# Row sums of one adjacency on ScalarE instead of TensorE, and the last two batches' h turned by exchange instead of by transposes

## The chip, the cores and the metric

The kernel runs on one core of a Trainium2 chip. The metric is the device time of one execution in microseconds (us). The engines are called as in the profile: PE is TensorE's matmul, PEld its weight load, ACT is ScalarE, DVE is VectorE, POOL is GpSimd, SP is SyncE, which here only issues DMAs (SPq in the profile).

## The reference

There are B = 16 graphs of N = 1024 nodes with C = 128 features, a 0/1 symmetric adjacency `adj[b]` for each, and L = 4 layers in each of two blocks.

```
# block 0: gated graph layers
h = relu(layernorm(x))
for i in 0..3:
    m = adj[b] (summed over nodes) of h @ weight[i]
    r = sigmoid(W_ir m + b + W_hr h + b);  z = sigmoid(W_iz m + b + W_hz h + b)
    n = tanh(W_in m + b + r * (W_hn h + b))
    h = (1 - z) * n + z * h
x = x + h * nodemask
# block 1: graph convolutions
h = relu(layernorm(x))
for i in 0..3:
    h = relu(adj[b] @ (h @ W[i]) + b[i])
    h = gamma[i] * (h - mean) * rsqrt(var + eps) + beta[i]     # over all batches and nodes
x = x + h
```

## The kernel before

Features lie on the 128 partitions and nodes along a row wherever a layer works (`hT`, 128x1024), nodes lie on the partitions where the layernorm works (`xt`, 8 blocks of 128x128). A product with the adjacency is written in two parts, a rounded high part of its operand and the rest, so one `aggregate` of a batch has 32 matmuls of 128x512 (L525): 8 rows of the adjacency, by two parts, by two halves of the nodes, into two PSUM banks.

**First phase** (block 0). Two streams, `sa` for the even batches and `sb` for the odd ones, take turns in `half_step(one, two)`. In each half step `one` aggregates (tiles `pm`) while `two` goes through its gates (`gate_step`, twelve pairs of matmuls at L969 into `g_r`, `g_hn`, `g_xn`, `g_z`, then sigmoid, tanh and the update of h on ACT and DVE). At the end of an aggregate, ACT copies both banks to `m` (L944). A counter `clock` starts at 3 and goes up by one in each half step. Side jobs are put in an agenda by `at(n, place, job)` and issued by `due(place)` in half step n; those of the place "gap" are issued in the middle of the aggregate. `plan` puts there, for one batch, the tail of the previous one and the preparation of the next. The order of all engines is written by hand for the first two half steps; for the rest of the phase only that of PE, POOL and SP is, and in the second phase a scheduler makes the order of all engines.

A batch's rows of the adjacency are loaded from the input as 32-bit values into `stage`, rounded into `row` tiles (`sa.rows` and `sb.rows`), and looked at for values that are not 0 or 1 by ACT: `glance` (L587) copies a row into `junk` while an accumulator sums it into `low`. POOL and a transposing DMA write the transposed adjacency in 16 bits to DRAM, `adjT_d[b]`, for the second phase.

**Tail of a batch.** h lies with features on the partitions, x with nodes. For all but the last two batches, `blocks_out` turns each half of h by one DVE transpose of 32x32 blocks (L711) into a `t_out` half tile and stores it by one SP DMA in DRAM (`cross_out`); a half step later `exchange_in` brings it back by four SP DMAs of 64 KB, which puts the blocks in their places; `tail_sums` adds it to x from SBUF, with the node mask (L732), and takes the layernorm's sums; `y_mid` is the normalized x (L674), and both go to DRAM (`xmid_d`, `ymid_d`). For batches 14 and 15, `last_tail` does it without the exchange: `tail_sums` has PE transpose the eight 128x128 blocks of h into PSUM (`pt_x`, L726), DVE adds from there, and `store_xmid` follows. What is left, `rest()`, is the normalizing and the store of y. For batch 14 `sa.rest()` is issued behind the last gates of batch 15, for batch 15 `sb.rest()` behind the second phase's first `first_weights`.

**Second phase** (block 1). Layer 0 runs over the 16 batches in order. `load_adjT` (L1229) loads eight rows of 256 KB each by SP DMAs, for an even batch into the one `block` tile, for an odd batch into `packed` half tiles, a ring of eight buffers that the first phase uses for `t_out`, `t_h` and the like. Each row is then widened to 32 bits (`wide`) by ACT (rows 1, 4 and 7, L1232) or by DVE (the others, L1234). `first_split` loads y from `ymid_d` and makes its high part on ACT (`chw`, L1291) and the rest on DVE (L1292). `aggregate` fills the banks `pc_m` (even batches) or `pc_g_r`, `pc_g_z` (odd ones), and `first_weights` of the batch before stands in TensorE's order between the aggregate's two halves or behind it: ACT copies the banks to `cm` (L1301), PE multiplies by the weights (`pw`, L1302), ACT makes `feat` (L1281). `work2` is a pool of the second phase that takes the place of the first phase's `work`, and `cm` is its first tile.

For the layers 1 to 3, batch 0 uses the sums of its adjacency's rows, `degree` (128x1024, the same in each partition, kept in the space of `w_mT`), in `raw_weights`. `row_sums` makes them on PE as a product of a matrix of ones with batch 0's `wide` rows (`pt_deg`, L1328), 16 matmuls behind batch 0's aggregate in the code, and ACT copies them from PSUM (L1332).

Of the kernel before, what the change touches and what calls it, by code (L numbers as in the profile page):

```python
# [8 lines left out]
F32 = mybir.dt.float32  # L9
F32R = mybir.dt.float32r  # L10
BF16 = mybir.dt.bfloat16
U16 = mybir.dt.uint16
I32 = mybir.dt.int32
AF = mybir.ActivationFunctionType
ALU = mybir.AluOpType
AX = mybir.AxisListType
P = 128
HALF = 512
# [323 lines left out]
def exact_path(  # L342
# [21 lines left out]
    nc = tc.nc  # L364
    B, N, C = x.shape
    L = g_weight.shape[0]
    NB = N // P
    NH = N // HALF
    BH = HALF // P
    assert C == P  # L370

    const = ctx.enter_context(tc.tile_pool(name="const", bufs=1))
# [9 lines left out]
    def tmp(name):  # L382
        return ps_t.tile([P, HALF], F32, tag="tmp", name=name)

    adjT_d = [dram.tile([NB, P, N], BF16, tag=f"adjT{b}", name=f"adjT_d{b}") for b in range(B)]
    xmid_d = [dram.tile([N, C], F32, tag=f"xmid{b}", name=f"xmid_d{b}") for b in range(B)]
    ymid_d = [dram.tile([P, N], F32, tag=f"ymid{b}", name=f"ymid_d{b}") for b in range(B)]

    def flat(name):
        return keep.tile([P, NB, C], F32, tag="x", name=name, bufs=4)  # L390
# [19 lines left out]
    nc.vector.memset(ones, 1.0)  # L410
    low = const.tile([P, (B + 2) * NB], F32, tag="low", name="low")
    nc.vector.memset(low, 0.0)

    w_c = const.tile([P, L, C], F32, tag="w_c", name="w_c")
    w_mT = const.tile([P, L, 3 * C], F32, tag="w_mT", name="w_mT")
# [118 lines left out]
    with ExitStack() as st:  # L534
# [46 lines left out]
        def glance(b, stage, js):  # L581

            junk = work.tile([P, N], BF16, tag="junk", name=f"junk{b}_{js[0]}", bufs=1)
            for j in js:
                lows = stage[j % 4].bitcast(U16).rearrange("p (n t) -> p n t", t=2)[:, :, 0]
                k = b * NB + j
                nc.scalar.activation(junk, lows, AF.Copy, accum_out=low[:, k : k + 1])  # L587

        def exchange_out(t, name):
            d = rawd.tile([P, HALF], F32, tag="cross", name=f"cross_{name}", bufs=8)  # L590
            nc.sync.dma_start(d, t)
            return d

        def exchange_in(d, t):

            src = d.rearrange("(t r) (s x) -> s r t x", t=4, s=4)
            for s in range(4):
                nc.sync.dma_start(t[s * 32 : (s + 1) * 32, :].rearrange("r (t x) -> r t x", t=4), src[s])  # L598
# [84 lines left out]
        def norm_apply(xt, y, nt):  # L683
            norm_root(nt, 0, NB)
            norm_scale(nt, 0, NB)
            norm_blocks(xt, y, nt, range(NB))
# [13 lines left out]
        def by_nodes(cols):  # L700
            return cols.rearrange("c (q k i) -> c k q i", q=4, i=32)

        def four_ways(cols):
            return cols.rearrange("p (k a c) -> p k a c", a=4, c=32)

        def blocks_out(src, name):

            return [half_out(cross_tile(f"t_{name}_{hf}"), src, hf, name)[0] for hf in range(NH)]
# [5 lines left out]
        def cross_tile(name):  # L714
            return half_tile(name).bitcast(F32)

        def tail_sums(b, xt, hT, parts=None):

            for hf in range(NH):
                if parts:  # L720
                    pt = by_nodes(parts[hf])
                else:
                    pt = tmp(f"pt_x{b}_{hf}")
                    for q in range(BH):
                        k = hf * BH + q
                        nc.tensor.transpose(pt[:, q * P : (q + 1) * P], hT[:, k * P : (k + 1) * P], ident)  # L726
                    pt = four_ways(pt)
                for q in range(BH):
                    k = hf * BH + q
                    xk = xt[:, k, :].rearrange("p (a c) -> p a c", a=4)  # L730
                    mask = maskT[:, b * NB + k : b * NB + k + 1]
                    nc.vector.scalar_tensor_tensor(xk, pt[:, q, :, :], mask, xk, ALU.mult, ALU.add)  # L732
            return norm_stats(xt, f"mid{b}")
# [5 lines left out]
        def y_mid(b):  # L739
            return work.tile([P, N], F32, tag="h", name=f"y_mid{b}", bufs=7)  # L740

        def store_xmid(b, xt):
            nc.gpsimd.dma_start(xmid_d[b].rearrange("(k p) c -> p k c", p=P), xt)
# [2 lines left out]
            nc.gpsimd.dma_start(ymid_d[b], y)  # L746

        def last_tail(b, xt, hT):
            nt = tail_sums(b, xt, hT)
            y = y_mid(b) if b + 1 < B else xt.rearrange("p k c -> p (k c)")  # L750
            store_xmid(b, xt)

            def rest():
                norm_apply(xt, y, nt)
                store_ymid(b, y)

            return rest
# [10 lines left out]
        class Stream:  # L768
# [53 lines left out]
            def plan(self, n, tail=None):  # L822

                if tail:
                    b, xt, hT, parts = tail
                    end = {}

                    def sums():
                        end["norm"] = tail_sums(b, xt, hT, parts)

                    def blocks():
                        end["y"] = y_mid(b)
                        norm_blocks(xt, end["y"], end["norm"], range(NB))

                    at(n + 2, "gap", sums)
                    at(n + 3, "mid", lambda: store_xmid(b, xt))
                    at(n + 3, "gap", lambda: norm_factors(end["norm"]))
                    at(n + 4, "gap", blocks)
                    at(n + 5, "mid", lambda: store_ymid(b, end["y"]))
                if self.b + 2 < B:  # L840
                    at(n + 5, "mid", self.next_load)
                    at(n + 5, "gap", self.next_sums)
                    at(n + 6, "gap", self.next_factors)
                    at(n + 7, "gap", self.next_blocks)
# [180 lines left out]
        def at(n, place, go):  # L1025
            agenda.setdefault((n, place), []).append(go)
# [5 lines left out]
        def half_step(one, two, gated=None, halfway=None):  # L1032

            feed.next_step()
            one.split = []
            if one.i == 0:
                two.fetch()
            due("ins")
            if one is sb and one.i == 0 or written[0] and one is sa:
                feed.jobs = transposes([(s.b, s.rows) for s in (sa, sb)])  # L1040
            if one.i > 0:
                one.split_step()
                two.fetch()
                feed.some(2)
            two.gate_step(0)
            two.half_away(0)
            two.first_four()
            if feed.full or (clock[0], "mid") in agenda:

                pace = small.tile([P, 1], F32, tag="pace", name=f"pace{clock[0]}")  # L1050
                nc.gpsimd.tensor_copy(pace, two.new[:, :1])
                feed.store()
                due("mid")
            due("outs")
            one.split_back(0, two.last_act, two.mid_dve)
            one.split_back(1, two.last_act, two.mid_dve)
            if one.i > 0:
                feed.some(1)
            two.gate_step(1, None, one.split)
            two.half_away(1)  # L1060
            with behind(two.first_act):
                due("late")
            if one.i == 0:
                feed.some(1)
            two.last_four()
            if gated:
                gated()
            if one.i == 0:
                with behind(two.last_m):
                    one.split_step()  # L1070
            one.agg_step(0)
            if halfway:
                halfway()
            with behind(two.last_act, two.last_dve, *one.split):
                due("gap")
            feed.some(NB if written[0] and one is sa else 1)
            one.agg_step(1)
            two.finish()
            clock[0] += 1
# [3 lines left out]
        with tc.tile_pool(name="prep", bufs=1) as prep, tc.manual_schedule(engines=every):  # L1083
# [106 lines left out]

            sa.plan(0)
            sb.plan(1)
            half_step(sa, sb, looks, lambda: turn_layer(prep, w_g, 1))
            join_layer(1)
            half_step(sb, sa, None, lambda: turn_layer(prep, w_g, 2))
# [124 lines left out]
            nc.tensor.matmul(pc[hf], w_c[:, i, :], mt[:, cols], start=True, stop=True)  # L1320
        conv_done(0, i, pc, stats)

    def row_sums(rows):

        pd = [tmp(f"pt_deg{hf}") for hf in range(NH)]
        for j in range(NB):
            for hf in range(NH):
                nc.tensor.matmul(  # L1328
                    pd[hf], ones_r, rows[j][:, hf * HALF : (hf + 1) * HALF], start=(j == 0), stop=(j == NB - 1)
                )  # L1330
        for hf in range(NH):
            nc.scalar.copy(degree[:, hf * HALF : (hf + 1) * HALF], pd[hf])  # L1332

    xo = []

    def pieces(b):
# [28 lines left out]
            for n0, n in pieces(k):  # L1365
                nc.gpsimd.dma_start(xo_piece(k, n0, n), by_node(xmid_d[k], n0, n))

    ones_r = work.tile([P, P], F32R, tag="ones_r", name="ones_r", bufs=1)
    nc.vector.tensor_copy(ones_r, ones.to_broadcast([P, P]))
    degree = w_mT.rearrange("p l c -> p (l c)")[:, :N]  # L1370

    stats = small.tile([P, B * NH, 6], F32, tag="bn_st", name="stats0")
# [1 line left out]
    for b in range(B):  # L1374
        rows = load_adjT(b, 0)
        hw_next = first_split(b + 1) if b + 1 < B else None
        pm = banks(b, 0)
        aggregate(pm, hw, rows, 0)
        if waiting:
            last = first_weights(*waiting, stats)  # L1380
            if b == 1:
                with tc.issue_after(last.ins):
                    sb.rest()
        if b == B - 1:
            hw_next = raw_split(1)
        aggregate(pm, hw, rows, 1)
        if b == 0:
            row_sums(rows)
        hw, waiting = hw_next, (b, pm)


# [110 lines left out]
```

## Time and profile before

| what | us |
|---|---|
| median of three runs | 1797.83 (1797.73 to 1798.45) |
| profiled execution | 1797.0 |
| its span | 1795.1 |
| PE busy | 1762.7 |
| ACT busy | 1108.3 |
| DVE busy | 1259.4 |
| POOL busy | 389.0 |

The mean clock granted to TensorE was 0.997 of full speed. The profiled execution has 1.9 us around its span and lies 0.83 us below the median of the runs. The first phase takes the span up to about 1175 us, the second the rest; the first layer of the second phase takes 9.02 us a batch from batch 2 on.

In the lines of a timeline or chain the first number is the start in the span, the second the duration, both in us; brackets hold the idle time of the engine before it and what ended it. Neighbouring instructions of one kind are one line (x8).

### The profile page before, as it was taken

Reading aid. Unit: us, or ns where it says so; the run is one execution under the profiler, and the core shown is the slowest. Engines: PE = TensorE matmul, PEld = TensorE weight load, DVE = VectorE, ACT = ScalarE, POOL = GpSimd, SP = SyncE. Lnnn points to the kernel's source line nnn. Section 1 sums busy time; section 2 is a strip of 40 time slices with the busy share of each in tenths; the row PEclk is TensorE's granted clock in tenths of the full one; section 3 lists DMA queues with packets and bytes.
Section 4 is the critical chain, followed back from the end, with each engine's and each line's share of the span. In section 5 each row is a group of like instructions: output and inputs, shape, how many; then the busy total and the mean of one; then the engine's idle time right before and its main releaser. Section 6 shows DMA issues by size and latency. Waiting matters only on the chain.

```text
span 1795.1 us, 22286 instructions
## 1 busy us (share of the span) xinstructions
PE 1762.7 (98%) x6742; PEld 1194.2 (67%) x6742; DVE 1259.4 (70%) x2307; ACT 1108.3 (62%) x1717; POOL 389.0 (22%) x417
## 2 busy tenths in 40 slices
PE   9999999999999999999999999999999999999997
PEld 6555555565566555656555655677778888888886
DVE  7567867877776776877686766676666666666665
ACT  5346557466556555655655645477777767768765
POOL 3213423332332331422332333010100000000010
PEclk9999999999999999999999999999999999999999
DMA  6447777676676766766866767778866565757666
GB/s 252 113 127 263 190 206 245 197 214 212 213 208 217 230 192 196 255 201 175 284 175 187 246 197 211 270 270 309 280 220 246 205 247 207 255 214 251 230 227 255
DMA packets 363968, 399.11 MB, mean 222 GB/s; under 512 B 159820, under 2 KB 240496, under 8 KB 363840
## 3 DMA queue, kind: packets, MB, share of 16 engines
q1 hardware_dynamic: 343088, 322.54, 56.9%
q0 software_dynamic: 20224, 74.80, 11.5%
q8 instruction: 55, 0.90, 0.2%
q14 instruction: 73, 0.60, 0.1%
q10 hardware_dynamic: 528, 0.26, 0.0%
HBM read 266.95 MB, written 96.99 MB: 203 GB/s over the span
## 4 chain that ended last, share of the span: by engine, by line
PE 81%; DMA 5%; DVE 5%; ACT 4%; issue 2%; SPq 2%; DVEq 0%; ACTq 0%
PE pm L525 20%; PE pc_m L525 13%; PE g_z L969 10%; PE g_r L969 9%; PE pc_g_z L525 6%; PE pc_g_r L525 6%; PE g_xn L969 5%; PE g_hn L969 5%; PE hw_c L500 4%; DMA cross_in<-t_in 1%; ACT y_in L674 1%; SPq L598 1%; DMA stage<-in_adj_dram 1%; DMA cross_h<-t_h 1%; PE pw_g_hn L1302 1%
## 5 line engine op out<-in xcount | busy, mean ns | idle before, releaser
L525 PE MATMUL pm<-row,ghw 128*128 128x512 f32 x2048 | 505.3, 403 | 10.7 <-ACT ghw L905 10.6
L525 PEld LDWEIGHTS pm<-row,ghw 128*128 128x128 f32 x2048 | 384.3, 188 | 123.1 <-issue 26.3
L525 PE MATMUL pc_m<-wide,chw 128*128 128x512 f32 x1024 | 246.0, 395 | 0.0
L609 POOL CAST half<-row 128x1024 bf16<-128x1024 f32 x128 | 147.9, 1163 | 329.0 <-DMA adjT<-half 314.2
L525 PEld LDWEIGHTS pc_m<-wide,chw 128*128 128x128 f32 x1024 | 190.4, 188 | 42.3 <-issue 4.3
L988 ACT ACTIVATE z<-g_z,brz 128x512 f32<-128x512 f32 x128 | 87.5, 684 | 172.6 <-PE g_z L969 172.3
L525 PE MATMUL pc_g_r<-wide,chw 128*128 128x512 f32 x464 | 186.9, 403 | 0.3 <-ACT chw L502 0.3
L578 POOL CAST row<-stage 128x1024 fp32r<-128x1024 f32 x112 | 132.9, 1196 | 241.0 <-DMA stage<-in_adj_dram 194.9
L525 PE MATMUL pc_g_z<-wide,chw 128*128 128x512 f32 x464 | 181.0, 390 | 0.0
L982 DVE SCALAR_TENSOR_TENSOR r<-g_hn,vecs,r 128x512 f32<-128x512 f32 x128 | 95.1, 743 | 121.4 <-ACT r L981 76.6
L944 ACT COPY m<-pm 128x512 f32<-128x512 f32 x128 | 68.5, 587 | 151.6 <-PE pm L525 151.6
L1234 DVE CAST wide<-block 128x1024 fp32r<-128x1024 bf16 x160 | 109.9, 692 | 73.2 <-PE pc_m L525 48.3
L1234 DVE CAST wide<-packed 128x1024 fp32r<-128x1024 bf16 x160 | 110.2, 691 | 72.0 <-PE pc_g_z L525 53.9
L987 ACT ACTIVATE r<-r,vecs 128x512 f32<-128x512 f32 x128 | 91.8, 717 | 100.7 <-DVE r L983 100.5
L994 DVE TENSOR_TENSOR h<-h,r 128x512 f32<-128x512 f32 x96 | 81.3, 847 | 98.4 <-ACT r L987 98.4
L1232 ACT CAST wide<-packed 128x1024 fp32r<-128x1024 bf16 x96 | 100.6, 1048 | 59.0 <-PE pc_m L525 26.6
L969 PE MATMUL g_r<-m,w_mT 128*128 128x512 f32 x256 | 131.3, 594 | 3.5 <-ACT m L944 3.2
L1232 ACT CAST wide<-block 128x1024 fp32r<-128x1024 bf16 x96 | 100.6, 1048 | 52.3 <-PE pc_g_z L525 27.7
L969 PE MATMUL g_xn<-m,w_mT 128*128 128x512 f32 x256 | 130.7, 592 | 0.0
L969 PE MATMUL g_z<-m,w_mT 128*128 128x512 f32 x256 | 130.7, 592 | 0.0
L995 DVE TENSOR_TENSOR h<-h,z 128x512 f32<-128x512 f32 x128 | 116.3, 912 | 4.6 <-ACT z L988 1.5
L1282 DVE BATCH_NORM_STATS2 stats<-feat 128x6 f32<-128x512 f32 x128 | 84.1, 686 | 47.0 <-ACT feat L1281 45.9
(186 smaller groups left out, 2808.2 us busy)
## 6 DMA issues: line engine op xcount, KB each, us to landing
block<-adjT_d SPq DMA_DIRECT2D x256, 256.0 KB, 4.7
packed<-adjT_d SPq DMA_DIRECT2D x256, 256.0 KB, 5.6
stage<-in_adj_dram SPq DMA_DIRECT2D x120, 512.0 KB, 5.1
adjT_d<-adjT POOLq DMA_DIRECT2D x16, 2048.0 KB, 8.3
cross_h<-t_h SPq DMA_DIRECT2D x90, 256.0 KB, 3.0
n_h<-cross_h SPq DMA_DIRECT2D x360, 64.0 KB, 2.0
xmid_d<-x POOLq DMA_DIRECT2D x16, 512.0 KB, 5.3
y<-ymid_d POOLq DMA_DIRECT2D x16, 512.0 KB, 5.3
```

The source lines that it names most:

```text
L525: nc.tensor.matmul(pm[hf], hw[s][:, j * P : (j + 1) * P], rows[j][:, hf * HALF : (hf + 1) * HALF], start=(j == 0 and s == 0), stop=(j == N ...
L578: nc.gpsimd.tensor_copy(t, stage[j % 4])
L609: nc.gpsimd.tensor_copy(t, row.bitcast(F32))
L969: nc.tensor.matmul(po, wT[:, i, g * C : (g + 1) * C], rhs, start=start, stop=stop)
L982: nc.vector.scalar_tensor_tensor(r, phn, b_hn(i), r, ALU.add, ALU.mult)
L987: nc.scalar.activation(r, r, AF.Tanh, bias=b_in(i))
L988: self.last_act = nc.scalar.activation(z, pz, AF.Sigmoid, bias=brz[:, 3 * i + 1 : 3 * i + 2])
L994: nc.vector.tensor_sub(ho, hin, r)
L995: nc.vector.tensor_mul(ho, ho, z)
L1232: nc.scalar.copy(r, t)
L1234: nc.vector.tensor_copy(r, t)
L1282: nc.vector.bn_stats(stats[:, b * NH + hf, :], dst)
```

## The change

Row sums: for each of the first four half steps, two of batch 0's rows are summed by ACT in the "gap" place, by a copy into `junk` with an accumulator, into a column of `deg` each (128x8). In the fifth, a POOL DMA stores `deg` as 1024 values in DRAM, `degree_d`, and at batch 0 of the second phase a POOL DMA loads them into all partitions of `degree`. The product with ones, its operand and the copies from PSUM are gone.

Tails: `last_tail` turns h by `blocks_out`, as the tails of other batches do, and everything else (the exchange back, the additions, the sums, the stores) goes into `rest()`. The branch of `tail_sums` that transposes on PE is gone.

```diff
+    degree_d = dram.tile([1, N], F32, tag="degree", name="degree_d")
...
+    deg = const.tile([P, NB], F32, tag="deg", name="deg")
...
+        def row_sums(rows, js):
+
+            junk = work.tile([P, N], BF16, tag="junk", name=f"total{js[0]}", bufs=1)
+            for j in js:
+                nc.scalar.activation(junk, rows[j].bitcast(F32), AF.Copy, accum_out=deg[:, j : j + 1])
+
...
-        def tail_sums(b, xt, hT, parts=None):
+        def tail_sums(b, xt, parts):
 
             for hf in range(NH):
-                if parts:
-                    pt = by_nodes(parts[hf])
-                else:
-                    pt = tmp(f"pt_x{b}_{hf}")
-                    for q in range(BH):
-                        k = hf * BH + q
-                        nc.tensor.transpose(pt[:, q * P : (q + 1) * P], hT[:, k * P : (k + 1) * P], ident)
-                    pt = four_ways(pt)
+                pt = by_nodes(parts[hf])
...
         def last_tail(b, xt, hT):
-            nt = tail_sums(b, xt, hT)
-            y = y_mid(b) if b + 1 < B else xt.rearrange("p k c -> p (k c)")
-            store_xmid(b, xt)
+            outs = blocks_out(hT, f"out{b}")
+            parts = [hT[:, hf * HALF : (hf + 1) * HALF] for hf in range(NH)]
 
             def rest():
+                for d, t in zip(outs, parts):
+                    exchange_in(d, t)
+                nt = tail_sums(b, xt, parts)
+                y = y_mid(b) if b + 1 < B else xt.rearrange("p k c -> p (k c)")
+                store_xmid(b, xt)
                 norm_apply(xt, y, nt)
                 store_ymid(b, y)
...
+            for k in range(4):
+                js = range(2 * k, 2 * k + 2)
+                at(3 + k, "gap", lambda js=js: row_sums(sa.rows, js))
+            at(7, "gap", lambda: nc.gpsimd.dma_start(degree_d.rearrange("o (k p) -> p (o k)", p=P), deg))
             half_step(sa, sb, looks, lambda: turn_layer(prep, w_g, 1))
...
-    def row_sums(rows):
-
-        pd = [tmp(f"pt_deg{hf}") for hf in range(NH)]
-        for j in range(NB):
-            for hf in range(NH):
-                nc.tensor.matmul(
-                    pd[hf], ones_r, rows[j][:, hf * HALF : (hf + 1) * HALF], start=(j == 0), stop=(j == NB - 1)
-                )
-        for hf in range(NH):
-            nc.scalar.copy(degree[:, hf * HALF : (hf + 1) * HALF], pd[hf])
...
-    ones_r = work.tile([P, P], F32R, tag="ones_r", name="ones_r", bufs=1)
-    nc.vector.tensor_copy(ones_r, ones.to_broadcast([P, P]))
...
         if b == 0:
-            row_sums(rows)
+            nc.gpsimd.dma_start(degree, degree_d.rearrange("o n -> (o n)").partition_broadcast(P))
```

More of the change, by code (lines that the diff above doesn't have):

```diff
@@ L828, in sums @@
                     def sums():
-                        end["norm"] = tail_sums(b, xt, hT, parts)
+                        end["norm"] = tail_sums(b, xt, parts)
                     def blocks():
```

## The prediction

> **What bounds the kernel now.** I read the page first, for the engine that fills the span and the chain that ended last.
>
> ```profile
> PE 1762.7 (98%) x6742; PEld 1194.2 (67%) x6742; DVE 1259.4 (70%) x2307; ACT 1108.3 (62%) x1717; POOL 389.0 (22%) x417
> ...
> PE 81%; DMA 5%; DVE 5%; ACT 4%; issue 2%; SPq 2%; DVEq 0%; ACTq 0%
> ```
>
> TensorE is busy for 98% of the span and 81% of the chain lies on it. Work taken off TensorE shortens the kernel unless a new wait fills the hole, so each step below is a walk along TensorE's queue. Second, the tile view of `pt_deg`, the product with ones, and the chain of waits around the change of phase, near 1162 to 1189 us (start, us, what):
>
> ```profile
> L1328 PE MATMUL pt_deg<-wide,ones_r x16: 387/391/467, 1184.7 to 1188.3; 128*128 128x512 f32 x16
> ```
>
> ```profile
> 1162.05 0.87 PE pt_x L726 x8
> ...
> 1173.92 0.44 PE pt_x L726 x4
> ...
> 1176.68 0.43 PE pt_x L726 x4
> ...
> 1183.67 1.07 ACT cm L1301 x2
> 1184.74 3.91 PE pt_deg L1328 x16
> ```
>
> Everything that the change removes from TensorE is on the chain. Third, ACT's timeline, for the holes that take the new row sums and for the order of work after the change of phase (start, us, idle before it and its end in brackets):
>
> ```profile
> 59.58 1.07 ACT L944 COPY m<-pm 128x512 f32<-128x512 f32 x2 [3.17 <-PE pm L525]
> 80.43 1.07 ACT L944 COPY m<-pm 128x512 f32<-128x512 f32 x2 [3.18 <-PE pm L525]
> 102.82 1.07 ACT L944 COPY m<-pm 128x512 f32<-128x512 f32 x2 [6.38 <-PE pm L525]
> 120.39 1.07 ACT L944 COPY m<-pm 128x512 f32<-128x512 f32 x2 [3.95 <-PE pm L525]
> ...
> 1161.67 1.06 ACT L1291 CAST chw<-y 128x1024 fp32r<-128x1024 f32 x1 [2.12 <-PE pm L525]
> 1162.63 1.06 ACT L944 COPY m<-pm 128x512 f32<-128x512 f32 x2
> ...
> 1176.65 3.19 ACT L674 ACTIVATE y_mid<-x,ms_mid,rs_mid 128x128 f32<-128x128 f32 x8 [0.99 <-DVE ms_mid L670]
> 1181.35 1.05 ACT L1291 CAST chw<-y 128x1024 fp32r<-128x1024 f32 x1 [1.51 <-PE pc_m L525]
> ```
>
> Last, SP's timeline, because the new exchanges are issued there, among the loads of the second phase's rows:
>
> ```profile
> 1146.35 3.88 SPq L1229 DMA_DIRECT2D block<-adjT_d  x8
> 1150.63 6.09 SPq L1229 DMA_DIRECT2D packed<-adjT_d  x8
> 1158.43 3.83 SPq L1229 DMA_DIRECT2D block<-adjT_d  x8
> 1162.62 24.25 SPq L1229 DMA_DIRECT2D packed<-adjT_d  x8
> ```
>
> Now batch 1's rows (the first `packed` group) are asked for at 1150.6 to 1156.7, some 25 us before TensorE needs them at 1181.6. That cover is what the change spends.
>
> **Removed.** The row sums: 3.91 us of TensorE. The 16 transposes of `pt_x`: by their neighbours' starts in TensorE's timeline 0.88, 0.36 and 0.35, so 1.59 us. `pt_flag` (0.12 us) moves far forward, to a place near 1060 us where TensorE waits 2.8 us anyway. Gross ceiling 5.6 us. The cast of `ones_r` (0.30 us DVE) and the two ACT copies of `degree` (1.06 us) go too, in places where neither ends a wait of TensorE.
>
> **Added early: nothing.** A row sum is an ACT copy of 128x1024 with an accumulator; the nearest row is `junk` (L587, 1.047 us and 0.187 us for reading the accumulator), so two per gap take 2.5 us, in gaps where ACT idles 3.17, 3.18, 6.38 and 3.95 us. 0.7 us to spare: TensorE's aggregate hides them. Without that cover it would be up to 4 x 2.5 = 9.9 us; I take 0. The store of `degree_d` is one issue on POOL (0.89 us for `adjT_d` at 130.86) before an idle stretch of 14.84 us. The load waits for w_mT's first layers, free since about 1136 us, is one issue of some 0.6 us on POOL with only `xo` loads behind it, and is first used at 1333 us: 0. No row has 4-byte elements; the nearest, the 64 KB exchange pieces in runs of 512 B, land in 2.0 us (up to 8.9), and 1000 us lie between store and load.
>
> The Trainium skill's page "DMA: Bandwidth & Descriptors" (Specifications) wants 512 B or more for line rate and says that smaller pieces are read, modified and written; the page would make this store slow, which the 1000 us hide as well.
>
> **Moved: the tail of batches 14 and 15.** The order on each engine is known, since the changed program can be built; durations are from rows of before.
>
> *First* (batch 14's eight transposes, 0.88 us): they cover ACT, which casts `chw` (1.06) before it copies m. Without them the two `g_r<-h` matmuls end at 1162.74 while the first m is there at about 1163.2. So 0.5 comes back; 0.36 stays. `pc_m` of batch 0 loses 0.71 and 0.12 more and ends at 1181.61 - 1.19 = 1180.4.
>
> *Second* (SP's queue): behind the first block loads stand now batch 14's two stores and eight pieces, and, after the first of batch 1's `packed` rows, batch 15's two stores. These wait for DVE's transposes of h, whose second half is finished at 1175.5 to 1176.1 (L996) and then needs a place on a DVE that also does batch 14's sums, and 0.70 us for the transpose. Batch 1's rows 1 to 7 are issued only from about 1177.8 and land, at the median of 5.1 us for L1229 (2.4 to 7.7; I take 3.4, as only the first must be in), from 1181.2. ACT meanwhile runs y_mid of 14 (3.19 us, about 1177.9 to 1181.1) ahead of row 1's cast (1.05): ready at 1182.2. TensorE comes to row 1 at 1180.4 + 0.9 = 1181.3 and stands 0.9 us. At the best 0; at a landing of 7.7 us, 4. It ends batch 1's aggregate at 1182.2 + 28 x 0.227 = 1188.6.
>
> *Third* (the copy cm of batch 0, which empties the banks for batch 2's aggregate and feeds TensorE's `pw`): it now stands on ACT behind `chw` of batch 3, which starts at the end of batch 1's aggregate (1188.9 to 1190.0), and its buffer is released only when DVE's last addition of batch 15's h to x is done. DVE has those additions on both sides of its low part of `chw` (1.23): 1190.0 + 1.23 + 4 x 0.34 = 1192.6. Then half of cm (0.5) and a wake-up: `pw` starts at 1193.5 instead of 1188.6. TensorE stands 4.9 us; behind it are `pw` and the whole of batch 2. At the best, were cm to wait for `chw` alone, 1.9. At the worst, batch 15's stores land in 6.9 us, the median of `cross_out`, instead of 3.0, the median of `cross_h`, and its additions end 1 to 4 us later. I take the small end in both, since at this point the first phase's stage loads are over.
>
> The Trainium skill's page "DMA: Bandwidth & Descriptors" (Anatomy of one DMA) gives a transfer, there one issued by GpSimd, about 2.0 us of fixed time whatever its size, plus bytes/436e3; as an estimate by that page one half's trip out and in is 2.6 + 2.15 = 4.75 us, against 5.0 to 8.9 by the rows, in place of four transposes of 0.44 us. It speaks against the change, and by it the sum stays as it is, as landings then are not the last to arrive.
>
> *Fourth*, after 1195 us ACT has x of batch 15 (3.19), cm and `feat` to catch up, with some 3 us free in each 9.02 us of a batch: batch 3's cm comes at about 1206.3, needed at 1207.9: 0 (at most 1.5).
>
> **Sum.** -0.36 - 0.71 - 0.12 - 3.92 = -5.1; +0.9 + 4.9 = +5.8; together +0.7: batch 2's aggregate starts at 1195.2 instead of 1194.56, and TensorE runs without a stop from there. The profiled execution took 1797.0 us (span 1795.1 and 1.9 around it), so 1797.7; the median of the three runs is 0.83 above it, and 1797.83 + 0.7 = 1798.5. About 0.2%, 3.6 us, is what a measurement of this kernel can tell from no change; that is two thirds of the whole gross gain.
>
> **Rivals.** *Full gain*: the new waits are covered (rows of batch 1 in time, cm early); for it speaks that TensorE is 98% busy and the removed work lies on the chain, against it the built order. -5.1: 1792.7. *Part of it*: cm waits only for `chw`: -5.1 + 0.9 + 1.9 = -2.3: 1795.5. *Slower*: one mechanism, SP's queue. Batch 1's rows stand behind stores that wait for DVE; it decides from a landing of over 4 us on. At 7.7 row 1 comes 3.5 to 4 us late instead of 0.9, all that follows shifts (chw of 3, additions, cm): +3.3 to +3.8, and with batch 15's pieces late too, +4 to +6: 1801.1 to 1804. For it: 5.6 us median of all `packed` loads on the page; against: block loads of 2.4 us exist. *The change does not do what it says* is excluded for the row sums (no PE product is left in the built program).
>
> **Chances.** As worked out 0.38 (1796 to 1801), part of the gain 0.12 (a third of it beyond 3.6 us), full gain 0.22, slower 0.28. Faster by over 0.2%: 0.22 + 0.04 = 0.26; within: 0.46; slower: 0.28. Range 1792.3 (just under full gain) to 1803.5.
>
> **What would show it.** In the changed profile: ACT's row sums in the four holes with m's copies no later; no `pt_deg`, no `pt_x`; SP's `packed` loads after the first one at 1177 us or later; TensorE idle before batch 1's row 1 by about 1 us on `wide`, and before `pw_g_hn` by about 5 us on `cm`. If that last wait is missing, I am wrong towards faster; if the `wide` wait has several us, towards slower; if m's copies near 60 to 120 us come later, the row sums are not free.

## The result and the profile after

The changed kernel takes 1816.97 us in the median of four runs (1814.22 to 1819.48), against 1797.78 for the kernel before on the same chip: a ratio of 1.0108, 95% interval 1.0093 to 1.0123. That is 19.2 us slower. The profiled execution has a span of 1815.1 us, 20.0 more than before. TensorE does less (32 matmuls fewer on the page), but its busy time is longer, as some of them ran at a lower clock:

```profile
PE 1766.1 (97%) x6710; PEld 1192.4 (66%) x6710; DVE 1254.9 (69%) x2310; ACT 1116.7 (62%) x1731; POOL 389.2 (21%) x419
```

To find the place, I laid the copies of m of the two traces side by side; each marks the end of an aggregate. Up to 138 us they stand at most 0.4 us apart, in the next half step 8.9, in the one after it 10.2. From there to the last aggregate of the first phase the distance stays between 9.2 and 11.0. Batch 2's aggregate in the second phase starts 18.4 us late, batch 3's 19.1. So there are two places: about 9.8 us near 150 us, and 8 us at the change of phase; the rest is spread thinly.

**The first place.** The store of the sums is the only new transfer there. From the view of DMA issues of the changed kernel for 110 to 190 us (KB, then us to landing):

```profile
adjT_d<-adjT POOLq DMA_DIRECT2D x1, 2048.0 KB, 17.8
...
degree_d<-deg POOLq DMA_DIRECT2D x1, 4.0 KB, 17.2
```

A store of 4 KB landed after 17.2 us, and the 2 MB store in front of it after 17.8 instead of 9.5 before. The windows view shows what happened to all else: for 140 to 150 us, first before, then after (the last two columns are the busy share of the DMA engines and GB/s):

```profile
140.00:150.00 10.00, 10.00 (x28) 5.02 (x27) 6.76 (x10) 7.04 (x13) 3.39 (x3) 1.00 0.75 260
```

```profile
140.00:150.00 10.00, 8.82 (x21) 3.61 (x19) 2.13 (x3) 2.67 (x4) 0.00 (x0) 1.00 0.92 42
```

The DMA engines are busier and move a sixth of the bytes. The h exchange of that half step and the stage loads behind it on SP come late, and TensorE waits twice, as its timeline after shows:

```profile
151.19 9.41 PE L527 MATMUL pm<-row,ghw 128*128 128x512 f32 x32 [2.37 <-ACT ghw L910]
...
165.07 1.64 PE L974 MATMUL g_r<-m,w_mT 128*128 128x512 f32 x2 [3.61 <-ACT m L949]
```

The waits are 6.0 us. Most of the rest is a clock that falls behind a wait: the aggregate takes 9.41 us instead of 7.84, and the granted clock was 0.83 between 150 and 160 us.

**The row sums themselves** stand in the holes as predicted, and they do not make m's copies late: the first copy behind them is 0.41 us behind the one before, the next three 0.35 to 0.40 (ACT's timeline after):

```profile
57.96 1.06 ACT L595 ACTIVATE total<-row 128x1024 bf16<-128x1024 f32 x1
58.93 0.19 ACT L595 ACTIVATION_READ_ACCUMULATOR total<-row 128x1 f32 x1
59.99 1.07 ACT L949 COPY m<-pm 128x512 f32<-128x512 f32 x2 [0.87 <-PE pm L527]
```

ACT even idles 0.87 us before the copy, the remainder of the 3.17.

**The second place** shows both waits that the prediction named, each longer. SP's and TensorE's timelines after:

```profile
1181.64 0.43 SPq L1238 DMA_DIRECT2D packed<-adjT_d  x1
1189.39 0.98 SPq L599 DMA_DIRECT2D cross_out<-t_out  x2
1190.42 3.32 SPq L1238 DMA_DIRECT2D packed<-adjT_d  x7
1193.84 5.59 SPq L606 DMA_DIRECT2D h<-cross_out  x8
```

```profile
1195.26 0.50 PE L527 MATMUL pc_g_r<-wide,chw 128*128 128x512 f32 x1 [3.03 <-ACT wide L1241]
...
1210.18 2.07 PE L1311 MATMUL pw_g_hn<-cm,w_c 128*128 128x512 f32 x2 [6.66 <-DMA packed<-adjT_d]
```

SP stands 7.3 us (1182.1 to 1189.4) in front of batch 15's stores, with batch 1's loads behind them. TensorE waits 3.03 us for row 1 and 6.66 for cm. The profile names a late `packed` load as the end of the second wait, but DVE and ACT show what came last: the fourth of batch 15's last additions ends at 1209.38, the copy cm starts at 1209.54.

```profile
1208.25 1.13 DVE L733 SCALAR_TENSOR_TENSOR x<-h,maskT,x 128x128 f32<-128x128 f32 x4
```

```profile
1209.54 1.07 ACT L1310 COPY cm<-pc_m 128x512 f32<-128x512 f32 x2 [5.35 <-DMA packed<-adjT_d]
```

After each of the two waits the granted clock is 0.66 for 5 us (1195 to 1200 and 1210 to 1215), and the four `pw` matmuls take 2.8 us from first start to the next aggregate instead of 1.3.

### The profile page after: what moved, and what is told of

Its sections match the earlier page's. It is cut to its first block, busy times and chain, and to the rows that moved or that the text cites. A ratio compares the mean times of both kernels' runs of the same rounds, so it can differ in the third digit from the quotient of the medians.

```text
span 1815.1 us, 22260 instructions
## 1 busy us (share of the span) xinstructions
PE 1766.1 (97%) x6710; PEld 1192.4 (66%) x6710; DVE 1254.9 (69%) x2310; ACT 1116.7 (62%) x1731; POOL 389.2 (21%) x419
```

## The experiments

Each ratio is against the kernel before, run on the same chip. The profiled executions of the variants differ by some us in the first phase without a cause that I could name: the first `pc_m` starts between 1172.7 and 1177.4 us in traces without a 4-byte store. What follows the last aggregate varies as well, by up to 2.1 us. So for the second phase I also give its length between the two, from the start of the first `pc_m` to that of the last sixteen `pc_g_z` matmuls: 1757.9 - 1172.7 = 585.2 us before and 1777.4 - 1183.4 = 594.0 after, 8.7 more. In the six traces that only add a store it stays within 0.1 us of before.

**The store alone, in the kernel before** (`store_4B`):

```diff
+    deg = const.tile([P, NB], F32, tag="deg", name="deg")
+    nc.vector.memset(deg, 0.0)
...
+            at(7, "gap", lambda: nc.gpsimd.dma_start(degree_d.rearrange("o (k p) -> p (o k)", p=P), deg))
```

> The kernel before with one thing more: a POOL DMA that stores 128x8 values of a constant tile as 1024 single 4-byte elements in DRAM, in the fifth half step, where the change has its store. Nothing reads it. Theory (the store): this DMA lands in about 17 us, all other transfers crawl meanwhile, the h exchange of that half step comes late, and the kernel is 9 to 11 us slower: about 1807.5. Rival (the store is innocent; the loss near 150 us comes from the row sums on ACT or from the order of POOL): within 1 us of before, 1797.8.

1810.0 us, ratio 1.0065 (1.0048 to 1.0082), landing after 18.3 us, 46 GB/s between 140 and 150 us. A transfer of 4 KB that nobody reads costs 12 us; in the trace the copies of m go from 0.5 to 9.1 us behind at this place, and the second phase is as long as before; the rest comes in the course of the first phase, without a cause shown. The rival falls.

**The row sums alone** (`sums_only`: the changed kernel with `last_tail` and `tail_sums` of before).

> The change's row sums alone, with the 4-byte store and the load of the degrees; the tails of batches 14 and 15 as before, by transposes on PE. Theory (store costs 10, product with ones was worth 3.9): 1797.8 + 10 - 3.9 = about 1804. If the store is innocent and the tails do all the harm: about 1794. If the row sums on ACT delay the gates in the first half steps as well: over 1806.

1806.03 us, ratio 1.0051 (1.0035 to 1.0068): the store's 12 less 4. The second phase is 4.0 us shorter than before: what the product with ones was worth.

**The tails alone** (`tails_only`: the kernel before with the changed `last_tail` and `tail_sums`).

> The change's tails of batches 14 and 15 alone; the row sums as before, by the product with ones on PE. In the changed kernel the stretch from the last aggregate of the first phase to batch 3 took 8.1 us longer than before although 3.9 us of product were gone. Theory (SP's queue and the cm wait): these waits remain, the product either adds its 3.9 (1797.8 + 12 = about 1810) or lies in the hole in front of pw (about 1806). Rival (waits come from the degree load's 512 KB in front): about 1797.

1805.94 us, ratio 1.0044 (1.0027 to 1.0061). The degree load isn't there, so it is not the cause. The time is that of a product lying in the hole, but the trace shows another reason for it: the product stands behind the hole. It starts after a wait of 5.99 us, when DVE has made its operand `ones_r` behind batch 15's last additions, and takes 6.24 us instead of 3.92, at a granted clock of 0.51 between 1195 and 1200 us (PE's and DVE's timelines):

```profile
1196.91 6.24 PE L1325 MATMUL pt_deg<-wide,ones_r 128*128 128x512 f32 x16 [5.99 <-DMA packed<-adjT_d]
```

```profile
1195.28 1.13 DVE L725 SCALAR_TENSOR_TENSOR x<-h,maskT,x 128x128 f32<-128x128 f32 x4
...
1196.60 0.21 DVE L1366 CAST ones_r<-ones 128x128 fp32r<-128x128 f32 x1
```

The second phase is 9.2 us longer than before: waits for rows of 1.20 and 0.46 us, this wait, 2.3 for the slow product, less 0.7 for the transposes that stood there.

The two losses (8.0 and 7.9 us) fall short of 19.2. In the second phase the parts, -4.0 and +9.2, nearly give the +5.8 of `after_runs` below, but the changed kernel has +8.7: its wait for row 1 is 3.03 us instead of 1.20 here and 1.33 there, with a slow stretch behind it. What made that wait longer is open.

**The sums in longer runs, tails as changed** (`after_runs`):

```diff
-            at(7, "gap", lambda: nc.gpsimd.dma_start(degree_d.rearrange("o (k p) -> p (o k)", p=P), deg))
+            def store_sums():
+                pt = tmp("pt_sums")
+                nc.tensor.transpose(pt[:NB, :P], deg, ident)
+                degT = work.tile([P, N], BF16, tag="junk", name="degT", bufs=1).bitcast(F32)[:NB, :P]
+                nc.scalar.copy(degT, pt[:NB, :P])
+                nc.gpsimd.dma_start(degree_d.rearrange("o (k p) -> (o k) p", p=P), degT)
+
+            at(7, "gap", store_sums)
```

> The changed kernel, but the sums are first transposed on PE (one 128x8 transpose in the fifth half step), copied by ACT into 8 partitions and stored as 8 runs of 512 B instead of 1024 of 4 B. Theory (the store): the loss near 150 us goes, about 10 us faster than the changed kernel: 1807. Rival (any store of this place, or the row sums): stays at 1817.

1806.24 us, ratio 1.0054 (1.0037 to 1.0070): 10.7 us less than the changed kernel. The store lands in 4.0 us. The second phase is 5.8 us longer than before, with waits of 1.33 us for row 1 and 7.31 for cm.

**What of the store is dear.** Five more stores, each alone in the kernel before, of the same constant tile: pieces of 32 B (128), of 16 B (256), half and an eighth of the 4-byte elements, and the 1024 of them two half steps later.

```diff
# store_32B
+ nc.gpsimd.dma_start(degree_d.rearrange("o (p k) -> p (o k)", p=P), deg)
# store_16B
+ nc.gpsimd.dma_start(degree_d.rearrange("o (h p k) -> p (o h) k", p=P, k=4), deg.rearrange("p (h k) -> p h k", k=4))
# store_half
+ nc.gpsimd.dma_start(degree_d[:, :HALF].rearrange("o (k p) -> p (o k)", p=P), deg[:, :BH])
# store_eighth
+ nc.gpsimd.dma_start(degree_d[:, :P].rearrange("o (k p) -> p (o k)", p=P), deg[:, :1])
# store_later: as store_4B, with at(9, ...)
```

> The kernel before with a store of the same 4 KB at the same place as in store_4B, but as 128 runs of 32 B. Theory (the price goes by the number of pieces, about 17 us for 1024): 128 pieces cost 2 us in the queues, the exchange comes hardly later: 0 to +1.5 us, about 1798 to 1799.5. Rival (anything under 512 B, or any POOL store at this place, blocks the queues): +8 to +12.

> The kernel before with half of store_4B's elements: 512 single 4-byte elements at the same place. Theory (by pieces): it lands in about 9 us behind the 2 MB of adjT_d instead of 18, the exchange is 4 to 5 us late, of which PE's gates cover some: +3 to +6, about 1801 to 1804. Rival (a fixed price of the mode): +12 as in store_4B, 1810.

> The kernel before with an eighth of store_4B's elements: 128 single 4-byte elements at the same place, as many pieces as store_32B has. Theory (the number of pieces counts): as in store_32B nothing near 150 us, 1797.5 to 1800. Rival (the size counts, a piece of 4 B is dear whatever the number): exchange late by several us, +5 or more, 1802 to 1806.

> The kernel before with store_4B's 1024 single 4-byte elements two half steps later, near 175 us, where POOL has no store of adjT_d in front of it. Theory (the pieces themselves slow all transfers for some 10 us): the DMA lands in 8 to 12 us, the stage loads and the exchange of that half step come late, +4 to +10: 1802 to 1808. Rival (the price comes only with the 2 MB store in front): lands in 2 to 5 us, 1797.5 to 1799.

> The kernel before with the same 4 KB at store_4B's place as 256 pieces of 16 B. Theory (any piece smaller than 32 B is dear): +8 to +12, about 1808. Rival (only single 4-byte elements are): within 2 us of store_32B, 1798 to 1800.

| store | pieces | ratio (95%) | to landing, us | GB/s, 140 to 150 us | m's copies fall back, us |
|---|---|---|---|---|---|
| store_4B | 1024 of 4 B | 1.0065 (1.0048 to 1.0082) | 18.3 | 46 | 8.6 |
| store_half | 512 of 4 B | 1.0049 (1.0034 to 1.0063) | 15.9 | 41 | 9.0 |
| store_eighth | 128 of 4 B | 1.0056 (1.0038 to 1.0073) | 15.1 | 42 | 9.2 |
| store_16B | 256 of 16 B | 1.0023 (1.0013 to 1.0034) | 10.5 | 169 | 1.7 |
| store_32B | 128 of 32 B | 1.0016 (1.0007 to 1.0025) | 8.9 | 254 | 0.0 |

The last column is the distance of m's copies from those of the kernel before at 173 us, less that at 138 us: what the store costs at its place. My theory of the number of pieces fell: 128 pieces of 4 B, half a kilobyte in all, cost as much as 1024 of them, and 128 pieces of 32 B nothing there (the 0.16% of that run lies elsewhere, without a cause shown). `store_half` was outside both expectations, nearer to the fixed price. The size of a piece counts. The windows of store_eighth and of store_32B:

```profile
140.00:150.00 10.00, 9.48 (x24) 3.92 (x22) 2.89 (x5) 3.22 (x5) 0.00 (x0) 1.00 0.48 42
```

```profile
140.00:150.00 10.00, 10.00 (x28) 4.99 (x27) 6.40 (x10) 6.49 (x12) 2.33 (x3) 1.00 0.75 254
```

1024 pieces of 4 B later (`store_later`), where no 2 MB store stands in front, land after 11.0 us and cost as much: 1807.16 us, 1.0048 (1.0036 to 1.0060), with TensorE waiting 7.00 us for the exchange (h_in) and m's copies falling back by 9.1. So the place is not the cause either. 16 B lies between, against both expectations.

**The second phase, wait by wait**, all with the sums stored in runs of 512 B as in `after_runs`. First, batch 15's h comes back into the half ring, so that cm's buffer does not wait for it (`runs_ring`):

```diff
-            parts = [hT[:, hf * HALF : (hf + 1) * HALF] for hf in range(NH)]
 
             def rest():
+                parts = [cross_tile(f"n_out{b}_{hf}") if b + 1 == B else hT[:, hf * HALF : (hf + 1) * HALF] for hf in range(NH)]
```

> The changed kernel with the store in 8 runs of 512 B; batch 15's h comes back into two tiles of the half ring instead of into its own place, so the first tile of the second phase's pool (cm) does not wait for the additions of batch 15; in the built order cm and pw of batch 0 then stand inside batch 1's aggregate again. Theory (cm's buffer waits for the tail): the wait of 7.3 us before pw and the slow pw behind it (1.7) go, what is left of row 1's wait stays: 1806.2 - 7 to 9 = about 1798. Rival (pw waits for late adjacency rows, as the profile names it): still about 1806.

1806.25 us, ratio 1.0040 (1.0024 to 1.0056). The wait before `pw` did shrink, from 7.31 to 0.59 us, so cm did wait for batch 15's additions, but the time did not: row 1's wait stood in its place.

```profile
1187.93 0.80 PE L527 MATMUL pc_g_r<-wide,chw 128*128 128x512 f32 x1 [3.04 <-ACT wide L1248]
...
1194.26 1.12 PE L1318 MATMUL pw_g_hn<-cm,w_c 128*128 128x512 f32 x2 [0.59 <-ACT cm L1317]
```

In `after_runs` row 1's wait was 1.33 us. Here it is 3.04: DVE's last transpose ends 2.6 us later, and with it SP issues batch 1's other rows later (1183.09 instead of 1180.45). The clock behind it is 0.50 from 1186 to 1191 us, and batch 3's row 1 waits another 2.15. The second phase is 6.4 us longer than before, no better than the 5.8 of `after_runs`.

Second, batch 15's two stores go to ACT's DMA queue (`runs_act`; `exchange_out` gets an `eng`, and `last_tail` passes `nc.scalar` for the last batch):

```diff
-            outs = blocks_out(hT, f"out{b}")
+            outs = blocks_out(hT, f"out{b}", nc.sync if b + 1 < B else nc.scalar)
```

> The changed kernel with the store in 8 runs of 512 B; batch 15's two stores are issued on ACT's DMA queue instead of SP's, so batch 1's packed loads stand right behind batch 14's pieces. Theory (two separate waits): row 1 no longer waits (1 to 3 us), but cm still waits for the additions of batch 15, which now get their pieces earlier: 1801 to 1805. Rival (SP's queue is the cause of all): 1796 or less.

1803.92 us, ratio 1.0037 (1.0024 to 1.0051). The time lies in the range of the theory of two waits, but the trace does not bear it out: against `after_runs` the waits for rows go from 1.33 only to 1.2 us in two parts, the one before `pw` is still 6.34, and the second phase is 5.8 us longer than before in both. The interval overlaps that of `after_runs`, too. That SP's queue is not the cause of all is shown; what it costs is not yet.

Third, both (`runs_both`).

> Both edits: batch 15's stores on ACT's queue and its h back into the half ring, with the store of the sums in 8 runs of 512 B. Theory: both waits of the second phase are gone or small, and what was predicted as the full gain is left: 1798.0 - 5 = about 1793; with one of them half there, 1795. Rival (the exchange itself, by its transfers beside the loads, costs): over 1797.

1802.05 us, ratio 1.0016 (1.0007 to 1.0024): neither the expected 1793 nor 1795. But the second phase is only 2.7 us longer than before. Batch 1 has no wait for rows any more, cm's is 1.08 us. Each edit alone gained nothing there (+6.4 and +5.8 against the +5.8 of `after_runs`), the two together 3.1. The step from `runs_ring` to `runs_both` shows SP's queue as a cause, as row 1's wait goes from 3.04 us to nothing. A third wait comes up: ACT stands before batch 15's normalizing, which writes in place of x, until the store of x has landed, and batch 3's row 1 stands behind that on ACT.

```profile
1205.30 3.19 ACT L682 ACTIVATE x<-x,ms_mid,rs_mid 128x128 f32<-128x128 f32 x8 [3.52 <-DMA xmid_d<-x]
```

```profile
1210.05 0.79 PE L527 MATMUL pc_g_r<-wide,chw 128*128 128x512 f32 x1 [3.52 <-ACT wide L1248]
```

Fourth, a buffer for that (`runs_y`):

```diff
-                y = y_mid(b) if b + 1 < B else xt.rearrange("p k c -> p (k c)")
+                y = y_mid(b) if b + 1 < B else work.tile([P, N], F32, tag="h", name=f"y_mid{b}", bufs=3)
```

> runs_both with one edit more: batch 15's normalized y goes to a tile of its own instead of in place of x, so ACT does not wait for the landing of the store of x. Theory: the 3.5 us wait before batch 3's row 1 (ACT stood behind that wait, and TensorE's clock fell to 0.65 behind it) goes: 4 to 5 us less than runs_both, so about 1797.5; with the first phase as in before, the second phase then has the predicted full gain and it would be 1793 to 1795. Rival (the wait moves to the next odd batch's rows, as it did before): 1801 to 1802.

1799.38 us, ratio 1.0003 (0.9993 to 1.0013), second phase 0.7 us longer than before. The 3.5 us are gone, small waits of 1.41, 0.95 and 0.28 us are left, the first of them with a slow `pw` behind it. The hoped-for 1793 to 1795 did not come: with three waits taken out, the turned tails cost what the row sums bring. That the exchange costs something by its transfers beside the loads, the rival named for `runs_both`, is not excluded for what is left.

**The row sums alone, stored in longer runs** (`sums_runs`: `store_sums` as above, `last_tail` of before).

> Row sums on ACT, stored as 8 runs of 512 B, tails as before by transposes on PE. Theory (only the 4-byte store did harm in this part): the product's 3.9 us are gained whole, less 0.1 for the transpose: 1798.0 - 3.8 = about 1794.2, 0.2% faster than before. Rival (the sums on ACT, or the load of degree into all partitions, cost something of their own): 1796 to 1798.

1794.91 us, ratio 0.9986 (0.9977 to 0.9995), second phase 3.9 us shorter than before. This version beats the kernel before by 3.5 us. The second phase gains all that the product took, so the load of `degree` into all partitions (9.7 us to landing) costs nothing that shows, and m's copies stay within 0.7 us of those before up to 210 us, so the sums on ACT and their store cost nothing that shows either.

## Why the prediction was wrong, point by point

**The store, taken at 0, was about 10 us.** This is the step that failed most. I priced the issue on POOL (0.89 us, and 0.89 it was) and asked who reads the result, 1000 us later. I did not ask what the transfer does to the others in the queues while it is under way. I took the nearest row for pieces of 4 B from pieces of 512 B, wrote down their landing of 2.0 us (up to 8.9), and used neither end, since the landing itself was hidden. The landing was hidden; the h exchange and the stage loads beside it were not. The tails were the second step to fail: without the store's loss, `after_runs` still takes 1806.24 us, above the 1803.5 that I gave as the upper end.

The Trainium skill's page "DMA: Bandwidth & Descriptors" (Specifications) names 512 B as the smallest piece for line rate, with a read, modify and write below it; I cited it as an effect on this store alone. The runs agree that small pieces are slow, but put the price otherwise: 32 B, well below the 512, cost 0.16%, none of it at the store's place, with a window of 254 GB/s; 4 B cost 0.5 to 0.65% whatever their number.

**The row sums on ACT, taken at 0: right.** So is the price of the product, 3.9 us; 4.0 and 3.9 us by the second phases of `sums_only` and `sums_runs`.

**The tails' two waits: the mechanism right, the sizes too small.** In the changed kernel row 1's wait was 3.0 us (0.9 predicted, at most 4), cm's 6.7 (4.9); without the 4-byte store they were 1.33 and 7.31. Row 1 was late because DVE was, and not because of its load, which landed 3.7 us after its issue (3.4 taken). DVE's additions for batch 14 began at 1179.62, after a wait of 1.74 us for the exchange's pieces, and stood among the updates of batch 15's h, so that the last transpose ended at 1190.0, and y_mid started at 1190.34, some 1.7 us later than in my walk shifted by the first phase's delay. In cm's case I had looked at the landing of batch 15's stores and taken the small end, 3.0 us, "since at this point the first phase's stage loads are over"; they landed in 2.0 and 2.6. What was late were the pieces coming back, which I had at 2.0 us: issued behind seven `packed` loads on SP, they took 5.9 to 9.2 us, up to 1205.9. The second phase's own loads had the DMA engines at 98 to 106% of their time from 1191 us on.

**The clock was left out.** Between the starts of batch 1's and batch 2's aggregates there are 21.88 us instead of 12.95. Without the product (-3.92), with the waits (+3.03 and +6.66), 3.2 us are left over, and they fall in the two stretches at a granted clock of 0.66. Before has no such stretch there, but it has one 100 us earlier, where I had noted the wait of 2.8 us: the aggregate behind it takes 9.46 us instead of 7.84, and the granted clock is 0.66 between 1065 and 1070 us. So the price of some 1.6 us for a wait of that size could be read, and it belonged into the upper bound. It does not always fall due: in `sums_runs` the aggregate behind the same wait, there 3.07 us, takes 7.85 us at a clock of 1.00 (PE's timelines, before and `sums_runs`).

```profile
1064.12 9.46 PE L525 MATMUL pm<-row,ghw 128*128 128x512 f32 x32 [2.85 <-ACT ghw L905]
```

```profile
1064.37 7.85 PE L527 MATMUL pm<-row,ghw 128*128 128x512 f32 x32 [3.07 <-ACT ghw L913]
```

The Trainium skill's page "TensorE: Matmul & The Clock Gate" (Part 1) tells of half the clock after an idle window of about 3.4 us; here a wait of 3.03 us was enough, and in `runs_y` one of 1.41 was followed by `pw` at 1.89 instead of 1.02 us for two matmuls.

**The rivals.** "Slower", at 0.28, had SP's queue and ended at 1804. That the queue is a cause is shown by `runs_both` against `runs_ring`, but not in the way that I made decisive, a landing of row 1 of over 4 us: it was issued late and landed in 3.7. And the rival had neither the store nor the clock. What is more, I called the likeliest case a near-cancellation (-5.1 and +5.8), in which each small miss of a wait counts whole. All four misses (store, two waits, clock) went the same way: here both waits that I had worked out from a profile without them came out too small.

**Open.** Why the first phase varies by some us from one kernel to the next, and why a piece of 4 B holds up the other transfers. That 16 B lie between 4 and 32 B fits a price by piece size, but no more than that is shown. The profile's packet counts do not help: each of the six stores adds 32 packets to queue q0 (20256 instead of 20224), whatever its pieces. All six were issued by POOL, and in all of them pieces of different partitions lie side by side in DRAM, so neither another queue nor pieces far apart were tried.

## What to carry to other kernels

Price a DMA by its smallest contiguous piece and by what shares the queues with it, not by its bytes or by when its result is needed; if the pieces are single elements, turn the tile first. When a step is moved off a full engine onto transfers, count the loads that stand behind its waits on the issuing queue, and the buffers that are released only when it ends: three such waits came up here; taking out either of the first two alone gained nothing, and taking out both showed the third. Take changes with two parts apart before keeping or dropping them: one half of this one, mended, is a gain of 0.14% (0.05 to 0.23).

## What the runs showed of the hardware that I had not expected

- A store of 128 single 4-byte elements (512 B in all) brought all transfers of the core from 260 to 42 GB/s for some 10 us and landed after 15.1 us; 1024 of them took 18.3. 128 pieces of 32 B in the same place left 254 GB/s.
- Waits of TensorE were often, but not always, followed by some us at half the granted clock. In the changed kernel the windows of 1 us read 0.50 from 1197 to 1199 us and 1.00 from 1200 on, behind the wait of 3.03 us; in `runs_y` the clock is 0.50 from 1191.5 to 1194 us behind a wait of 1.41; in `sums_runs` it stays at 1.00 behind one of 3.07. The 6.0 us of waits near 150 us cost some 3.4 us more in this way, the 9.7 us at the change of phase 3.2.
